# The row of scores stored word by word, and eight more state products in single passes, in a four-layer graph network under a planned order

## The chip, the cores and the metric

The kernel runs on one core of one Trainium2 chip. The metric is the device time of one execution in microseconds (us).

## The reference

There are 32 graphs of 512 nodes with 128 features each, and one weighted adjacency `adj` of 512 x 512 that all of them share. Four layers follow each other, each as x = x + layer(relu(layernorm(x))):

```python
# layer 0: normalised graph convolution
A = adj + eye;  d = A.sum(-1) ** -0.5
x = x + ((d[:, None] * A * d[None, :]) @ h) @ W.T + b
# layer 1: gated graph network, 5 steps
m_in = m_out = adj @ h;  av = concat(m_in, m_out);  u3 = h @ u3_w.T + u3_b
z = sigmoid(av @ w3.T + b3 + u3);  r = sigmoid(av @ w4.T + b4 + u3)
hv = tanh(av @ w5.T + b5 + (r * h) @ u5.T + u5b)
h = (1 - z) * h + z * hv
# layers 2 and 3: graph attention (elu after layer 2)
h = x @ W;  e = leaky_relu((h @ a_src)[:, None] + (h @ a_dst)[None, :], 0.2)
x = x + softmax(where(adj > 0, e, -inf)) @ h
```

All arithmetic is float32.

## The kernel before

**Order.** Nothing is scheduled by the compiler. The kernel first describes its work as some thousands of operations, each with an engine, an estimated cost, a delay until its result can be used, the values it reads and writes, and a due time (`op(engine, cost, due, emit, r, w, delay)`). `Plan.run` then simulates six queues (PE, DVE, ACT, POOL, SP, and ACT's DMA queue). In `attempt`, whenever an engine comes free, the ready operation with the earliest time that finds its buffers is started. The order in which operations were started is the order in which they are emitted. The times come from the due times or from a pass backwards (`ends` holds pairs of a last time and a factor for that), and `nudge` shifts them by pseudo-random amounts, one set for each number in the list `NUDGES`. On the chip every engine works through its own instructions in that order, and waits for semaphores where something is not there yet.

**Stages.** A graph b starts at due time 5 b (in units of one step); up to `LANES = 6` graphs are in the gated network at once, so layers 0, 1, 2 and 3 of different graphs overlap all the time. A tile of one graph is [128 partitions, 4 blocks, 128].

**Exact products from single passes.** A float32 matmul is an exact product (L829, function `weigh`), two records in the trace for 512 columns. Where `split` holds, an operand is cut into `upper` (ACT, L686), `lower` (DVE, L687) and `across` (DVE, L689) by `operands`, and the product is the sum of three matmuls in fp32r (L713 for adj, L832 for the gates), with a rescaling of the bank by ACT between two of them (L695). In `step`, the product of the state hT with the gate weight u3 is done this way for the pairs (batch, step) of `STATE_GATES`, and exactly for the others.

**Transposed copies.** States and features are turned by DVE in blocks of 32 x 32 (`sq`, L664 and L674) and rearranged by a shuttle through DRAM: four stores of 32 partitions (L667, L676) and a load (L669, L679), all issued from SP. Results are added onto x by accumulating DMAs from POOL (L658).

**Attention** (`gat`). Two pairs of matmuls (L962) give, for each node, 128 features and three scores; ACT takes the exponentials of the scores into columns D to D+2 of the tile `h_gat` (L978), then scales the features by column D (L982). The last column, D+2, holds what every destination node needs from every source node, and must become one row of 512 numbers that is the same on all partitions. For the 28 batches before the last four ("near") that goes through DRAM: DVE transposes the last 32 columns of `h_gat` into `four` (L998), one DMA stores one row out of every 32 partitions to `line` in DRAM (L1000), and a second loads `line`, broadcast over 128 partitions, into `row` (L1002). Then DVE builds the attention weights `e` (L1005, four per graph and layer) from row, column D+1 and the mask, and TensorE mixes (L1031). The near batches make their row on TensorE (L992) and mix at L1017.

The functions that the diff touches, with their line numbers:

Of the kernel before, what the change touches and what calls it, by code (L numbers as in the profile page):

```python
# [16 lines left out]
P = 128  # L17
# [3 lines left out]
W = 32  # L21
Q = P // W
# [5 lines left out]
RUN_UP = 8  # L28
LANES = 6
WHOLE_GATES = {(0, 0), (1, 0)}  # L30
STATE_GATES = {(b, s) for b in range(2, 32) for s in (1, 2, 3) if s > 1 or b % 4 == 1}

NUDGES = (
    53937, 420269, 836905, 654738, 2556, 688223, 875681, 275050, 155096, 344911, 330173, 435081, 694231, 213763,
    619624, 447574, 890946, 78316, 123147, 852796, 311235, 532539, 705019, 644762, 122001, 254734, 428857,
    882175, 724559, 991387, 688947, 809908, 194618, 494830, 529850, 799901, 343325, 398127, 50886, 241542,
    734658, 18633, 943566, 750849, 361157, 207391, 729651, 26139, 37696, 408480, 215591, 995383, 816582, 584268,
    494753, 34361, 342059, 302953, 168035, 239750, 279141, 68953, 280704, 389122, 194085, 766091, 380916,
    187191, 889942, 112078, 155070, 333073, 736484, 517839, 70535, 334845, 651590, 758394, 921455, 429200,
    648202, 752373, 775521, 430492, 606178, 231202, 882688, 679159, 354420, 928437, 520287, 661997, 81128,  # L40
    762603, 72380, 63081, 983120, 327354, 210125, 648122, 266391, 656086, 635831, 781379, 551997, 170768,
    229958, 7605, 122665, 19790, 73379, 142730, 998949, 708013, 923384, 153267, 690409, 481837, 535551, 726547,
    6387, 549650, 56134, 483951, 926497, 198992, 426418, 278155, 699450, 83978, 319322, 141756, 196198, 650583,
    862777, 201601, 166009, 204473, 988478, 570561, 164420, 526913, 618467, 275849, 776494, 261229, 110220,
    498182, 380461, 378001, 220860, 670765, 118796, 827070, 785629, 894747, 990151, 807156, 873672, 718913,
    239396, 50887, 63051, 862147, 532718, 800211, 505997, 9798, 801159, 13694, 618014, 193111, 44188, 893667,
    599496, 714567, 888600, 835938, 364887, 158288, 309678, 793120, 699620, 516755, 592013, 992036, 487540,
    190584, 971338, 58993, 486501, 268529, 250721, 557238, 569064, 166944, 933806, 390862, 463360, 136662,
    215430, 595978, 384591, 96926, 326923, 708222, 859934, 514585, 669817, 296375, 269747, 738262, 834297,
    459159, 608570, 133902, 490320, 941827, 144497, 573319, 819458, 309171, 845111, 880350, 927808, 432234,  # L50
    556385, 655493, 972795, 866892, 892882, 338341, 731096, 806800, 593721, 754374, 280850, 287395, 593450,
    812363, 340434, 322205, 340551, 845735, 66582, 645768, 736844, 878238, 109388, 497625, 999333, 437014,
    859840, 92294, 458622, 403652, 881921, 496809, 361450, 302403, 643048, 262383, 321316, 875159, 728173,
    763887, 249514, 200508, 52886, 149934, 537415, 299931, 655951, 358934, 513673, 678761, 726703, 828099,
    359414, 939210, 916234, 209320, 71814, 960653, 167324, 81204, 557783, 235008, 861486, 815903, 314980,
    593693, 811661, 356673, 912853, 833145, 889341, 728473, 302959, 14483, 119625, 907405, 192404, 98679, 42557,
    675297, 874633, 738462, 562610, 653446, 648327, 99334, 956314, 305909, 318958,
)


# [29 lines left out]
class Plan:  # L90
# [13 lines left out]
    def op(self, engine, cost, due, emit, r=(), w=(), delay=None):  # L104
        o = Op(engine, cost, due, emit, self.DELAY[engine] if delay is None else delay)
        o.id = len(self.ops)
        before = {}
        for items, writes in ((r, False), (w, True)):
            for item in items:
                v, parts = item if isinstance(item, tuple) else (item, None)  # L110
                parts = range(len(v.writers)) if parts is None else [parts]
                if v not in o.vals:
                    o.vals.append(v)
                    v.uses += 1
                for c in parts:
                    before.update((p.id, p) for p in v.writers[c])
                    if writes:
                        before.update((p.id, p) for p in v.readers[c])
        for items, writes in ((r, False), (w, True)):
            for item in items:  # L120
                v, parts = item if isinstance(item, tuple) else (item, None)
                for c in range(len(v.writers)) if parts is None else [parts]:
                    if writes:
                        v.writers[c], v.readers[c] = [o], []
                    else:
                        v.readers[c].append(o)
        before.pop(o.id, None)
        for p in before.values():
            p.then.append(o)
        o.waits = len(before)  # L130
        self.ops.append(o)
# [190 lines left out]
def gnn_stack(ctx: ExitStack, tc: tile.TileContext, a: dict, out: bass.AP):  # L322
    nc = tc.nc
    x, adj = a["x"], a["adj"]
    B, N, D = x.shape
    C = N // P
# [6 lines left out]
    def tiles(n, shape, name, pool=sb, dtype=F32):  # L333
        return [pool.tile(shape, dtype, name=f"{name}_{next(serial)}") for _ in range(n)]

    def flat(t):
# [19 lines left out]
        "hv": tiles(0, TOKENS, "hv"),  # L356
        "gT": tiles(0, [P, Q, W * C], "gT"),
        "h_gat": tiles(3, [P, C, D + 3], "h_gat"),
        "four": tiles(2, [P, Q, W], "four"),
        "row": tiles(2, [P, N], "row"),  # L360
        "line": tiles(4, [C, Q, W], "line", dram),
        "e": tiles(2, [P, C, N], "e"),
# [7 lines left out]
        "rstd": tiles(8, SMALL, "rstd"),  # L370
        "off": tiles(6, SMALL, "off"),
        "rden": tiles(3, SMALL, "rden"),
    }, [(167, 0.1), (181, 0.05)], 12,
        IDLE_FROM, lambda v: nc.tensor.transpose(v.t[:, 0, :], ident.t, ident.t))
    op = plan.op
    MM, MM1, TURN, MR = 0.858, 0.224, 0.111, 0.2325
# [44 lines left out]
    for c in range(C):  # L421
        e, q = (("ACT", nc.scalar), ("SP", nc.sync))[c % 2]
        op(e, 0.45, -1001, lambda c=c, q=q: q.dma_start(adj_sb.t[:, c, :], adj[c * P:(c + 1) * P, :]),
           w=[adj_sb[c]], delay=(3.2, 4.7, 4.4, 4.9)[c])
# [42 lines left out]
    for m in range(C):  # L467
        op("DVE", 0.26, -800 + 0.7 * m, lambda m=m: nc.vector.tensor_add(diag.t[:, m, :], block(adjT.t, m), ident.t),
           r=[adjT, ident], w=[diag[m]])
# [63 lines left out]
    for k, u, half in (("w4", "u3", True), ("w3", "u3", True), ("w5", "u5", False)):  # L533
        gate_b[k] = fixed([P, 1], "gate_b" + k)
        op("DVE", 0.1, -14, lambda k=k, u=u: nc.vector.tensor_add(gate_b[k].t, raw["b" + k].t, raw["b" + u].t),
           r=[raw["b" + k], raw["b" + u]], w=[gate_b[k]])
# [4 lines left out]
    for i, l in enumerate((2, 3)):  # L541
        p = Val("bank")
        op("PE", 0.3, 9, lambda i=i, l=l, p=p: nc.tensor.matmul(p.t[:, 0, :2], gats.t[:, i, :], a_pair[l].t, start=True, stop=True),
           r=[gats, a_pair[l]], w=[p])
# [138 lines left out]
    def operands(src, given, made, due):  # L683

        upper, lower, across = Val("upper"), Val("lower"), Val("across")
        op("ACT", COPY, due - 5, lambda: nc.scalar.mul(made(upper.t), given(src.t), BELOW), r=[src], w=[upper])  # L686
        op("DVE", V, due - 5, lambda: nc.vector.tensor_sub(made(lower.t), given(src.t), made(upper.t).bitcast(F32)),  # L687
           r=[src, upper], w=[lower])
        op("DVE", V, due - 5, lambda: nc.vector.scalar_tensor_tensor(  # L689
            flat(across.t), flat(lower.t).bitcast(F32), -SPLIT, flat(upper.t).bitcast(F32), op0=ALU.mult, op1=ALU.add),  # L690
           r=[lower, upper], w=[across])
        return upper, lower, across
# [131 lines left out]
    def step(b, s, m, hT, due, lane):  # L824
# [44 lines left out]

        if split and (b, s) in STATE_GATES:  # L870
            by_m(gate, 1, due + 0.2, True, parts=operands(hT, flat, flat, due))
# [69 lines left out]
    def gat(b, l, due):  # L941
        xb, y, gT, h = xs[b], Val("y", C), Val("sq"), Val("h_gat", 4)
# [13 lines left out]
        for a, q in enumerate(qs):  # L956
# [20 lines left out]
            else:  # L977
                op("ACT", 0.1, due + 1, lambda qt=qt, ht=ht: nc.scalar.activation(ht()[:, :, D:D + 3], qt()[:, :, D:D + 3], AF.Exp),  # L978
                   r=[q], w=[h[2 + a]])
# [4 lines left out]
        exps = [h[2], h[3]]  # L984

        row, e, mask = Val("row"), Val("e", C), (own_mask if near else maskT)[l]
        if near:
            pr = Val("bank")

            def spread():  # L990
                for k in range(Q):
                    nc.tensor.transpose(pr.t[:, k, :], h.t[:, k, D + 2:D + 3].to_broadcast([P, P]), ident.t)  # L992
            op("PE", C * TURN, due + 2, spread, r=[*exps, ident], w=[pr, e])
            row = pr
        else:

            four, line = Val("four"), Val("line")
            op("DVE", 0.2, due + 1.5, lambda: nc.vector.transpose(  # L998
                four.t, h.t[:, :, D + 3 - W:]), r=[h], w=[four])
            op("SP", 0.4, due + 1.5, lambda: nc.sync.dma_start(  # L1000
                line.t, four.t[W - 1::W]), r=[four], w=[line], delay=2.5)
            op("SP", 0.4, due + 1.5, lambda: nc.sync.dma_start(  # L1002
                row.t, line.t.rearrange("c q i -> (c q i)").unsqueeze(0).to_broadcast([P, N])), r=[line], w=[row, e], delay=7)
        for j in range(C):
            op("DVE", 0.661, due + 3, lambda j=j: nc.vector.scalar_tensor_tensor(  # L1005
                e.t[:, j, :], matrix(row), h.t[:, j, D + 1:D + 2], mask.t[:, j, :], op0=ALU.max, op1=ALU.mult),
               r=[row, h[2 + j // 2], mask], w=[e[j]])
# [4 lines left out]
        if near:  # L1012
# [7 lines left out]
            for js, cs in [([j], range(C)) for j in range(2 if apart else C)] + [((2, 3), [c]) for c in range(C if apart else 0)]:  # L1020
                op("PE", len(js) * len(cs) * MM1, due + 4, lambda js=js, cs=cs: mix_from(js, cs),
                   r=[part for j in js for part in (e[j], h[j // 2], h[2 + j // 2])], w=[*ps] if len(js) == 1 else [ps[cs[0]]])
# [36 lines left out]
        elif l == 2:  # L1059
            op("ACT", 0.505, due + 4, lambda: nc.scalar.activation(flat(n.t), flat(v.t), AF.Exp, bias=-1.0), r=[v], w=[n])  # L1060
            op("DVE", V, due + 4, lambda: nc.vector.scalar_tensor_tensor(flat(v.t), flat(n.t), 1.0, flat(v.t), op0=ALU.min, op1=ALU.max),  # L1061
               r=[n], w=[v])
# [13 lines left out]
    def attention(pair):  # L1076
        for b in (pair, pair + 1):
            gat(b, 2, STEPS * b + LANES * (STEPS - 1) + 3)
            gat(b, 3, STEPS * b + LANES * (STEPS - 1) + 8)
# [46 lines left out]
```

## Time and profile before

| | |
|---|---|
| median of 3 runs | 1486.99 us (1486.86 to 1487.59) |
| the profiled execution | 1487.39 us, of which span 1485.6 us |
| granted TensorE clock | 1.00 |
| idle of TensorE, VectorE, ScalarE, GpSimd in the span | 7.5, 79.4, 214.1, 823.1 us |
| DMA packets | 307,502, 196 MB |

The span is from the first to the last instruction of the profiled execution; 1.8 us lie around it. PE is TensorE's matmuls, PEld its weight loads, which overlap them; DVE is VectorE, ACT ScalarE, POOL GpSimd, SP the engine that issues most DMAs, and SPq its queue. A group's line gives source line, engine, operation, what is written and read, shapes and count, then busy time and the mean of one, and the engine's idle time just before, with what ended it. A wait's line has the waiter, the one waited for, then total us, times and the longest. A chain's line has start, length and what ran.

### The profile page before, as it was taken

The numbers are of one execution on the slowest core, as the hardware profiler recorded it, in microseconds if no ns is written. First come the engines' busy times: TensorE is split into PE (matmuls) and PEld (weight loads), VectorE is DVE, ScalarE is ACT, GpSimd is POOL, SyncE is SP. The second block draws the span as 40 slices with busy tenths as digits, with TensorE's granted clock in tenths as the row PEclk, the third lists the DMA queues.
The fourth block names the chain that finished last, engine by engine and source line by source line (L and its number), as shares of the span: only waits on it lengthen the run. The fifth ranks groups of instructions, "written<-read, shape, count | busy, mean of one in ns | idle before, by whom it ended". The sixth has DMA issues, their size and how long they took to land.

```text
span 1485.6 us, 25858 instructions
## 1 busy us (share of the span) xinstructions
PE 1478.1 (99%) x7481; PEld 1171.1 (79%) x7481; DVE 1406.2 (95%) x2951; ACT 1271.5 (86%) x2858; POOL 662.5 (45%) x1270
## 2 busy tenths in 40 slices
PE   9999999999999999999999999999999999999999
PEld 7777777787777788778778787877777877778888
DVE  8989999999998999899999999999999999999998
ACT  6978998888988888988889989799888889988874
POOL 5613641333755363655455553366536632414221
PEclk9999999999999999999999999999999999999999
DMA  3445555666766666666766557676576665553233
GB/s 107 65 104 144 108 127 117 139 142 159 154 136 134 156 156 138 139 142 138 178 138 145 134 128 153 143 173 139 127 162 154 148 158 122 136 135 74 70 79 79
DMA packets 307502, 196.12 MB, mean 132 GB/s; under 512 B 87872, under 2 KB 259232, under 8 KB 307360
## 3 DMA queue, kind: packets, MB, share of 16 engines
q1 hardware_dynamic: 276160, 157.24, 41.6%
q0 software_dynamic: 30912, 36.71, 16.3%
q8 instruction: 59, 0.97, 0.3%
q14 instruction: 83, 0.68, 0.2%
q10 hardware_dynamic: 288, 0.52, 0.1%
HBM read 87.30 MB, written 70.37 MB: 106 GB/s over the span
## 4 chain that ended last, share of the span: by engine, by line
PE 97%; DVE 1%; ACT 0%; DMA 0%; issue 0%; ACTq 0%; DVEq 0%
PE bank L713 35%; PE bank L832 26%; PE bank L829 15%; PE bank L1031 13%; PE bank L962 4%; PE bank L791 2%; PE bank L1017 2%; PE bank L736 1%; PE bank L653 0%; DVE e L1005 0%; DMA e<-in_adj_dram 0%; PE bank L507 0%; PE bank L992 0%; DVE st L630 0%; PE bank L455 0%
## 5 line engine op out<-in xcount | busy, mean ns | idle before, releaser
L695 ACT ACTIVATE bank<-bank 128x512 f32<-128x512 f32 x662 | 381.1, 598 | 92.4 <-PE bank L713 56.8
L689 DVE SCALAR_TENSOR_TENSOR across<-lower,upper 128x512 fp32r<-128x512 f32 x413 | 276.5, 678 | 2.2
L832 PE MATMUL bank<-upper,gates 128*128 128x512 f32 x541 | 257.2, 475 | 0.0
L1031 PEld LDWEIGHTS bank<-h_gat,e 128*128 128x128 f32 x1792 | 218.3, 191 | 17.6 <-issue 9.8
L1031 PE MATMUL bank<-h_gat,e 128*128 128x129 f32 x1792 | 220.5, 275 | 0.0
L832 PE MATMUL bank<-across,gates 128*128 128x512 f32 x541 | 218.3, 445 | 0.1
L832 PE MATMUL bank<-lower,gates 128*128 128x512 f32 x541 | 214.1, 396 | 0.0
L658 POOL DMA_DIRECT2D x<-y x80 | 72.1, 905 | 311.4 <-DVE y L1061 88.1
L713 PE MATMUL bank<-adj,upper 128*128 128x512 f32 x640 | 185.8, 412 | 0.0
L713 PE MATMUL bank<-adj,across 128*128 128x512 f32 x640 | 183.8, 411 | 0.0
L713 PE MATMUL bank<-adj,lower 128*128 128x512 f32 x640 | 172.7, 391 | 0.0
L829 PE MATMUL bank<-r,wT 128*128 128x512 f32 x320 | 163.3, 592 | 0.0
L1005 DVE SCALAR_TENSOR_TENSOR e<-row,h_gat,maskT 128x512 f32<-128x512 f32 x224 | 156.9, 741 | 0.0
L568 POOL TENSOR_TENSOR apart<-st 128x4 f32<-128x4 f32 x104 | 53.7, 517 | 218.1 <-DVE st L580 216.1
L713 PEld LDWEIGHTS bank<-adj,across 128*128 128x128 f32 x640 | 117.1, 188 | 36.6 <-issue 8.1
L713 PEld LDWEIGHTS bank<-adj,upper 128*128 128x128 f32 x640 | 117.8, 188 | 34.7 <-issue 10.3
L713 PEld LDWEIGHTS bank<-adj,lower 128*128 128x128 f32 x640 | 120.2, 188 | 26.6
L832 PEld LDWEIGHTS bank<-upper,gates 128*128 128x128 f32 x541 | 102.0, 188 | 42.5 <-issue 14.6
L832 PEld LDWEIGHTS bank<-across,gates 128*128 128x128 f32 x541 | 100.3, 188 | 41.1 <-issue 10.1
L874 ACT ACTIVATE r<-bank,gate_bw 128x512 f32<-128x512 f32 x160 | 111.4, 699 | 24.1 <-PE bank L829 21.4
L832 PEld LDWEIGHTS bank<-lower,gates 128*128 128x128 f32 x541 | 102.1, 189 | 37.8 <-issue 19.1
L568 POOL TENSOR_TENSOR rstd<-rstd,mhalf 128x4 f32<-128x4 f32 x104 | 128.1, 1232 | 5.1
(168 smaller groups left out, 3317.1 us busy)
## 6 DMA issues: line engine op xcount, KB each, us to landing
far<-sq SPq DMA_DIRECT2D x936, 64.0 KB
h<-far SPq DMA_DIRECT2D x148, 256.0 KB
x<-y POOLq DMA_DIRECT2D x80, 256.0 KB, 4.2
sq<-far SPq DMA_DIRECT2D x56, 256.0 KB
row<-line SPq DMA_DIRECT2D x56, 256.0 KB
adjT<-y POOLq DMA_DIRECT2D x32, 256.0 KB, 4.3
hT<-far SPq DMA_DIRECT2D x120, 64.0 KB
x<-in_x_dram SPq DMA_DIRECT2D x24, 256.0 KB
```

The costliest lines, as they stand in the source:

```text
L568: op("POOL", cost, due, lambda: nc.gpsimd.tensor_tensor(to(), one(), other(), how), r=r, w=w)
L658: op("POOL", 1.0, due, lambda: nc.gpsimd.dma_start(x.t, what(), accum_op=ALU.add), r=reads, w=[x], delay=7)
L689: op("DVE", V, due - 5, lambda: nc.vector.scalar_tensor_tensor(flat(across.t), flat(lower.t).bitcast(F32), -SPLIT, flat(upper.t).bitcast(F ...
L695: op("ACT", COPY, due, lambda: nc.scalar.mul(flat(p.t), flat(p.t), by), w=[p])
L713: nc.tensor.matmul(flat(p.t), left.t[:, c, :], right.t[:, c, :], start=first and c == 0, stop=c == C - 1, skip_group_check=True)
L791: nc.tensor.matmul(p.t[:, c, :], m.t[:, c, :], w0T.t[:, 0, :], start=True, stop=True)
L829: nc.tensor.matmul(flat(p.t), (of or gates).t[:, i, :], flat(moving.t), start=start, stop=True, skip_group_check=True)
L832: nc.tensor.matmul(flat(p.t), of.t[:, i, :], flat(moving.t), start=start, stop=True, skip_group_check=True)
L874: op("ACT", A, due - 5, lambda: nc.scalar.activation(flat(r.t), flat(gate.t), AF.Tanh, bias=gate_b["w4"].t, scale=0.5), r=[gate, gate_b["w ...
L962: nc.tensor.matmul(qt()[:, c, :D + 3], gT.t[:, 2 * a + c, :], w_aug[l].t, start=True, stop=True)
L1005: op("DVE", 0.661, due + 3, lambda j=j: nc.vector.scalar_tensor_tensor(e.t[:, j, :], matrix(row), h.t[:, j, D + 1:D + 2], mask.t[:, j, :], ...
L1031: nc.tensor.matmul(pt()[:, c, :D + 1], e.t[:, j, i * P:(i + 1) * P], h.t[:, j, :D + 1], start=(j == 0), stop=(j == C - 1))
```

## The change

Three things change in the text of the kernel.

1. `STATE_GATES` takes in step 1 of every odd batch, where it had every fourth: 75 pairs for 67.
2. In `gat`, for the batches that are not near, `four`, its buffers and the DVE transposition go. In their place four DMAs, one for each 32 partitions, read column D+2 straight from `h_gat` and store 128 single words each to a part of `line`. They need the exponentials alone, not the scaled features. The load of `row` is as it was, and waits for all four.
3. The planner's inputs: a store costs 0.44 and has a delay of 3, for 0.4 and 2.5; `ends` has one pair for two; `NUDGES` is another list, about half as long. So the order of the instructions differs on every engine.

```diff
-STATE_GATES = {(b, s) for b in range(2, 32) for s in (1, 2, 3) if s > 1 or b % 4 == 1}
+STATE_GATES = {(b, s) for b in range(2, 32) for s in (1, 2, 3) if s > 1 or b % 2}

 NUDGES = (
...
-        "four": tiles(2, [P, Q, W], "four"),
...
-    }, [(167, 0.1), (181, 0.05)], 12,
+    }, [(165.5, 0.090)], 12,
...
-            four, line = Val("four"), Val("line")
-            op("DVE", 0.2, due + 1.5, lambda: nc.vector.transpose(
-                four.t, h.t[:, :, D + 3 - W:]), r=[h], w=[four])
-            op("SP", 0.4, due + 1.5, lambda: nc.sync.dma_start(
-                line.t, four.t[W - 1::W]), r=[four], w=[line], delay=2.5)
+            line = Val("line", C)
+            for c in range(C):
+                op("SP", 0.44, due + 1.5, lambda c=c: nc.sync.dma_start(
+                    line.t[c].rearrange("q i -> i q"), h.t[c * W:(c + 1) * W, :, D + 2]), r=exps, w=[line[c]], delay=3)
             op("SP", 0.4, due + 1.5, lambda: nc.sync.dma_start(
                 row.t, line.t.rearrange("c q i -> (c q i)").unsqueeze(0).to_broadcast([P, N])), r=[line], w=[row, e], delay=7)
```

## The prediction

> **What bounds the kernel now.** I read the page first (busy shares, then the chain that ended last), then the stretches of time, then the groups of instructions.
>
> ```profile
> PE 1478.1 (99%) x7481; PEld 1171.1 (79%) x7481; DVE 1406.2 (95%) x2951; ACT 1271.5 (86%) x2858; POOL 662.5 (45%) x1270
> PE 97%; DVE 1%; ACT 0%; DMA 0%; issue 0%; ACTq 0%; DVEq 0%
> 0.00:50.00 50.00, 47.02 (x250) 36.55 (x250) 44.69 (x162) 37.20 (x81) 30.03 (x75) 1.00 0.34 90
> 1300.00:1400.00 100.00, 100.00 (x509) 78.86 (x508) 96.13 (x188) 85.56 (x192) 26.07 (x49) 1.00 0.41 100
> 1400.00:1440.00 40.00, 39.06 (x279) 34.41 (x278) 36.20 (x110) 31.48 (x94) 13.24 (x25) 1.00 0.31 73
> 1440.00:1486.00 46.00, 42.08 (x377) 41.79 (x375) 40.72 (x136) 24.62 (x88) 7.47 (x7) 1.00 0.28 70
> ```
>
> In the stretch lines the columns are the stretch, its length, then busy time and count of PE, PEld, DVE, ACT and POOL, granted clock, DMA share, GB/s. TensorE is idle 7.5 us in the whole span: 3.0 in the first 50, 0.9 in 1400 to 1440, 3.9 at the very end, and practically nothing between. The chain says the same: 97% is TensorE. Since busy ends of matmuls are modelled, I count as well. The chain has "81 us: 16 passes in 3.73 us", 0.233 us a pass of 512 columns:
>
> ```profile
> 80.96 3.73 PE bank L713 x16
> 711.97 0.23 PE bank L832
> 712.20 0.86 PE bank L829 x2
> 713.06 0.45 PE bank L962 x4
> ```
>
> There are 2,256 + 1,623 single passes (L713, L832), x 0.233 = 904 us; 518 records of L829, two to a product of 0.86, make 222; the other 3,058 records (3,026 at 0.11, 32 wider) make 349. The sum, 1,475, leaves 10.6 us of the 1485.6 for every gap, seven of them at the two ends. So only two things can move the time: TensorE's own work, and new gaps in it. Nothing that frees another engine is worth anything by itself.
>
> **What the Trainium skill says.** "FP8 and Floating Point Precision", TensorE Precision Notes: true FP32 takes four passes through the array. The trace agrees: 0.86 us for a product at L829 against 0.233 for a single pass, a ratio of 3.7. "DMA: Bandwidth & Descriptors", Rules for kernel authors: a non-contiguous last dimension lowers to one descriptor per element. No transfer of scores in this trace is of that kind, so only the new one will show it. The same page, Anatomy of one DMA, puts most of a fixed 2 us down to the receipt of the write; here the row copy follows the issue of its store by 1.6 us at the least and 2.8 in the median (56 pairs, from start times). "TensorE: Matmul & The Clock Gate", specifications: VectorE's queue is strictly first in, first out; in the trace it shows as stalls of whatever stands first (27.7 us of L687 behind L686).
>
> **Part 1, eight more state products in single passes.** STATE_GATES grows from 67 to 75 entries: step 1 of batches 3, 7, 11, 15, 19, 23, 27 and 31. Each loses one exact product and gains three single passes plus the split of hT.
>
> ```profile
> L829 PE MATMUL bank<-hT,wT 128*128 128x512 f32 x186 | 94.9, 592 | 0.0
> L686 ACT ACTIVATE upper<-hT 128x512 fp32r<-128x512 f32 x67 | 43.6, 653 | 1.9 <-DVE hT L890 1.9
> L687 DVE TENSOR_TENSOR lower<-hT,upper 128x512 fp32r<-128x512 f32 x67 | 45.3, 678 | 0.9 <-ACT upper L686 0.9
> L998 DVE STREAM_TRANSPOSE four<-h_gat 128x128 f32<-128x128 f32 x56 | 16.7, 298 | 2.9 <-ACT h_gat L982 2.9
> L1005 DVE SCALAR_TENSOR_TENSOR e<-row,h_gat,maskT 128x512 f32<-128x512 f32 x224 | 156.9, 741 | 0.0
> ```
>
> TensorE: 8 x (0.86 - 3 x 0.233) = 8 x 0.16 = **1.3 us less**, all of it on the path. ScalarE: 8 x 0.653 = 5.2 us more, on an engine with 214 us idle. VectorE: 16 splits x 0.678 = 10.8 us more (L687, L689). The rescaling of the bank is there already and isn't doubled. The first half of the gate now waits for a three-step split, about 2 us when nothing queues, before its passes; the other five lanes and the attention products cover that, as they do for the 67 splits of today: TensorE's waits before L832 for L687 and for L689 come to 0.5 us each. If that cover goes, up to 2 us x 8 = 16 us; I take 0, both ends kept.
>
> **Part 2, the row of scores.** Removed: 56 VectorE transpositions, 16.7 us, and the wait of the transposition on both scalings (2.9 us). VectorE in sum: 1406.2 + 10.8 - 16.7 = 1400.3 us, 6 less. Worth 0 on the path, as TensorE doesn't wait for VectorE. On SP, 56 stores of 0.500 us go (28 us) and 224 of one word per descriptor come. The nearest row is the shuttle's store, also 128 descriptors, 0.438 us in the median: 98 us. SP's issue records sum to 697 us, and become 767 of 1485.6. What SP loses as well is its wait on the transposition:
>
> ```profile
> SPq L1000 <- DVE four L998: 81.3, 22, 12.9
> SPq L1002 <- DMA line<-four: 22.4, 18, 2.6
> L1000 SPq DMA_DIRECT2D line<-four x56: 487/500/747, 216.0 to 1447.8; - x56
> ```
>
> Behind those 81.3 us stand the shuttle's transfers (L667, L669) that bring the states back, so a shorter wait is a help to them; four stores in place of one hold them up 4 x 0.438 - 0.5 = 1.25 us per row. Both fall inside the shuttle's slack, since waits for DMA hardly occur on the compute engines, and count 0. POOL's accumulating transfers only take other places; POOL is idle 55% of the span.
>
> The DMA engines get 56 x 512 = 28,672 packets of 4 bytes. The trace's packets of 128 bytes took 13.2 ns each and its 4-byte semaphore writes 9.1. At 13.2 it is 378 us over 16 engines, 24 us each, 1.6% of the span on engines busy some 58% in all. If a word cost as much as a 512-byte packet (31.5 ns), it would be 3.8%. Both are covered.
>
> How late does the row come? Before: issue 0.5, at least 1.6 to the row copy. After: issue 1.75 in all, then the last store's landing, which no row shows: between 1.1 us (as now, 1.6 less the 0.5 of issue) and, as a bound, 5 us, twice the longest wait that L1002 now has for it (2.6). It starts earlier by the scaling and the transposition: the store follows the second exponential (L978) by 2.3 us in the median, and that can fall to nothing. Before 2.3 + 1.6 = 3.9 us, after 1.75 + 1.1 = 2.9 to 1.75 + 5 = 6.8: between 1 us earlier and 2.9 us later. I take 0. Today L1005 has 0.0 us of idle before it, and starts 8.0 us (median; 4.9 at least) after the row copy is issued.
>
> **Part 3, other due times.** They redraw the order on all engines. With 10.6 us of gaps in all, of which about 3 are start and 4 are the last VectorE steps and stores, at most some 3 us are to be had, and any amount to be lost. I take 0, with -2 to +8.
>
> **Sum.** 1487.4 (the profiled execution: span 1485.6 and 1.8 around it) - 1.3 = 1486.1. The median of the three runs, 1486.99, is 0.4 below that execution: **1485.7**.
>
> **The cases.**
>
> A, 53%: as summed, order as tight as now: 1485.7, own range 1484 to 1489. For it: TensorE has no gap from 50 to 1400 us to begin with, and both engines that could starve it get no more work than they had, or little.
>
> B, 17%: the row arrives after the place where the order has L1005, VectorE stalls with everything behind it, and VectorE becomes the bound. Its room is 1484.3 - 1400.3 = 84 us, 1.5 us per row. A mean stall over 1.5 us decides; at 1.65, within the bounds above, 92 us of stalls give 84 + 8 over: 1485.7 + 8 = 1494. Against it: 4.9 us between copy and use at the worst today.
>
> C, 20%: the new order is looser, and splits come late for their passes (part 1). Of the bound of 16 us a third gives 5: 1485.7 + 5 = 1490.7, which I take; half gives 1493.7. It decides from 4.3 us of new gaps on. Against: the 67 splits of today work unseen.
>
> D, 10%: the new order also closes 1.5 to 2 us at the ends, 1483.9. For it: 0.9 us idle in 1400 to 1440 needn't be there. Against: the ends hang on first loads and last stores.
>
> That the change does less than it says can be left out: all eight pairs pass the condition in step() that chooses the split, and the counts would show it.
>
> **Numbers.** About 0.2% (3 us) is what a measurement of this kernel can tell from no change. Faster by more than that needs under 1484.0: D nearly whole and a sliver of A, 0.12. Slower means over 1490.0: B, most of C and A's rim, 0.35. The rest, 0.53, is no difference. The range runs from 1483.5 to 1494.5, leaving out the far ends of B, C and D.
>
> **What would show it.** Right: L829 for hT x170 instead of x186, L832 groups x549 each, no L998; TensorE busy all through 50 to 1400; span about 1484.3; L1005 still with no idle. Case B: idle before L1005 released by a DMA row. Case C: idle before L832 or L713 released by ScalarE or VectorE. I am wrong in kind if TensorE's counts are as said and the span moves by more than 3 us.

## The result, and the profile after

The changed kernel takes 1623.3 us (median of 4 runs, 1617.9 to 1628.8) against 1487.2 of the kernel before: a ratio of 1.0916, 95% interval 1.0889 to 1.0942. That is 136 us slower, far outside the range of the prediction. The profiled execution took 1621.3 us, its span 1619.5.

From the page of the changed kernel, the engines' busy times, the DMA count, and the chain that ended last by engine and by line:

```profile
PE 1522.4 (94%) x7487; PEld 1189.0 (73%) x7487; DVE 1407.9 (87%) x2911; ACT 1278.7 (79%) x2866; POOL 643.6 (40%) x1270
...
DMA packets 339311, 196.14 MB, mean 121 GB/s; under 512 B 119904, under 2 KB 291040, under 8 KB 339168
...
PE 41%; DMA 26%; ACT 13%; DVE 10%; SPq 6%; issue 3%; DVEq 0%; ACTq 0%
PE bank L701 14%; PE bank L820 10%; DMA line<-h_gat 7%; DMA h<-far 7%; PE bank L817 6%; DMA far<-sq 5%; PE bank L1018 5%; DMA sq<-far 5%; ACT bank L683 3%; ACT upper L674 2%; PE bank L950 2%; SPq L655 2%; SPq L987 2%; DVE lower L675 2%; DVE e L992 2%
```

Every engine is busy for a smaller share of the span than before. TensorE is idle for 97.1 us of the span where it was idle for 7.5, and busy for 44 us more. TensorE's share of the chain fell from 97% to 41%, and a quarter of the chain is now transfers: the new word stores (`line<-h_gat`, 7%) and, with more weight together, the three kinds of the shuttle that the change didn't touch. From the view of waits of the changed kernel, first the compute engines', then SP's own queue (waiter, waited for, us in total, times, longest):

```profile
ACT upper L674 <- DMA h<-far: 57.3, 24, 6.2
PE bank L950 <- DMA sq<-far: 39.6, 17, 6.9
DVE sq L652 <- DMA far<-sq: 31.9, 14, 6.7
DVE e L992 <- DMA row<-line: 22.0, 13, 5.5
```

```profile
SPq L989 <- DMA line<-h_gat: 136.4, 57, 6.6
SPq L655 <- DMA line<-h_gat: 33.5, 20, 4.0
SPq L664 <- DMA line<-h_gat: 17.7, 9, 3.2
```

Before, L1002 waited 22.4 us for its store; the same copy, now L989, waits 136.4. From the list of DMA issues of the changed kernel (KB of each, median us from issue to landing):

```profile
far<-sq SPq DMA_DIRECT2D x936, 64.0 KB, 2.8
line<-h_gat SPq DMA_DIRECT2D x224, 0.5 KB, 7.1
```

A store of 512 bytes in single words takes 7.1 us to land (the trace tells the landing of 31 of the 224), where a store of 64 KB takes 2.8. The planner was told 3 for it.

The first reading of this was theory S: the words land late, the row copy waits for them on SP, and everything behind it on that queue is late. Its rivals: theory E, the words hold up the DMA engines for every transfer, whoever waits; theory O, the new order is bad in itself. The experiments keep the changed kernel's order of instructions wherever they can, because the order alone turned out to be worth tens of us.

### The profile page after: what moved, and what is told of

The parts are those of the page before. It is cut to its first block, busy times and chain, and to the rows that moved or that the text cites. A ratio compares the mean times of both kernels' runs of the same rounds, so it can differ in the third digit from the quotient of the medians.

```text
span 1619.5 us, 25988 instructions
## 1 busy us (share of the span) xinstructions
PE 1522.4 (94%) x7487; PEld 1189.0 (73%) x7487; DVE 1407.9 (87%) x2911; ACT 1278.7 (79%) x2866; POOL 643.6 (40%) x1270
## 4 chain that ended last, share of the span: by engine, by line
PE 41%; DMA 26%; ACT 13%; DVE 10%; SPq 6%; issue 3%; DVEq 0%; ACTq 0%
PE bank L701 14%; PE bank L820 10%; DMA line<-h_gat 7%; DMA h<-far 7%; PE bank L817 6%; DMA far<-sq 5%; PE bank L1018 5%; DMA sq<-far 5%; ACT bank L683 3%; ACT upper L674 2%; PE bank L950 2%; SPq L655 2%; SPq L987 2%; DVE lower L675 2%; DVE e L992 2%
## 5 line engine op out<-in xcount | busy, mean ns | idle before, releaser
L677 DVE SCALAR_TENSOR_TENSOR across<-lower,upper 128x512 fp32r<-128x512 f32 x421 | 281.8, 679 | 3.2 <-PE bank L701 0.7
L820 PE MATMUL bank<-upper,gates 128*128 128x512 f32 x549 | 262.6, 478 | 7.8 <-ACT bank L683 4.3
L820 PE MATMUL bank<-across,gates 128*128 128x512 f32 x549 | 226.2, 455 | 5.4 <-ACT bank L683 5.1
L820 PE MATMUL bank<-lower,gates 128*128 128x512 f32 x549 | 221.9, 404 | 7.6 <-DVE lower L675 7.4
L1018 PE MATMUL bank<-h_gat,e 128*128 128x129 f32 x1792 | 223.9, 276 | 2.1 <-DVE e L992 1.4
L701 PE MATMUL bank<-adj,upper 128*128 128x512 f32 x640 | 193.7, 425 | 5.6 <-ACT upper L674 5.6
L992 DVE SCALAR_TENSOR_TENSOR e<-row,h_gat,maskT 128x512 f32<-128x512 f32 x224 | 156.5, 742 | 22.2 <-DMA row<-line 22.0
L675 DVE TENSOR_TENSOR lower<-h,upper 128x512 fp32r<-128x512 f32 x158 | 107.2, 679 | 53.1 <-ACT upper L674 51.8
L674 ACT ACTIVATE upper<-h 128x512 fp32r<-128x512 f32 x158 | 100.7, 638 | 62.7 <-DMA h<-far 57.3
L820 PEld LDWEIGHTS bank<-upper,gates 128*128 128x128 f32 x549 | 105.5, 192 | 52.7 <-issue 14.9
L820 PEld LDWEIGHTS bank<-lower,gates 128*128 128x128 f32 x549 | 105.5, 192 | 51.3 <-issue 18.2
```

Of the source, the lines that this page charges most:

```text
L701: nc.tensor.matmul(flat(p.t), left.t[:, c, :], right.t[:, c, :], start=first and c == 0, stop=c == C - 1, skip_group_check=True)
L820: nc.tensor.matmul(flat(p.t), of.t[:, i, :], flat(moving.t), start=start, stop=True, skip_group_check=True)
L1018: nc.tensor.matmul(pt()[:, c, :D + 1], e.t[:, j, i * P:(i + 1) * P], h.t[:, j, :D + 1], start=(j == 0), stop=(j == C - 1))
```

## The experiments

**1. The row copy doesn't wait.**

```diff
 op("SP", 0.4, due + 1.5, lambda: nc.sync.dma_start(
-    row.t, line.t.rearrange("c q i -> (c q i)").unsqueeze(0).to_broadcast([P, N])), r=[line], ...
+    row.t, adj[0:1, :].to_broadcast([P, N])), r=[line], ...
```

> The changed kernel, its order of instructions untouched on every engine; only the row copy reads a line of the adjacency in DRAM instead of the stored scores, so it no longer waits for the word stores (the scores are left out of the attention weights). All 224 word stores are still issued. Theory S (the single words land late, 7.1 us where the order allows 3.4, and the row copy that waits for them holds up everything behind it on SP): 136 us of SP's waits go, and the time falls by at least half of the 136 us of loss, to 1490 to 1555; what is left are the 75 us in which other transfers wait for the word stores. Theory E (the words clog the 16 DMA engines for all transfers): it stays over 1590. Theory O (the new order is bad in itself): it stays over 1590.

Measured: 1636.0 us (1631.9 to 1640.1; ratio 1.0999, 1.0966 to 1.1031). Nothing came back, though the row copy hardly waits any more. But its wait went in part to others. From SP's waits of experiment 1:

```profile
SPq L655 <- DMA line<-h_gat: 60.4, 34, 5.2
SPq L989 <- DMA line<-h_gat: 12.5, 11, 4.2
```

In sum SP waits 121 us for word stores, where it waited 211. So the wait of the row copy falls as the main cause; that SP is held up at other places by the late words isn't excluded by this run.

**2. Few words.**

```diff
-    line.t[c].rearrange("q i -> i q"), h.t[c * W:(c + 1) * W, :, D + 2]), r=exps, ...
+    line.t[c].rearrange("q i -> i q")[:1], h.t[c * W:c * W + 1, :, D + 2]), r=exps, ...
```

> The changed kernel in the same order, but each store takes 1 partition instead of 32: 4 words in place of 128, 16 in place of 512 a row (most of the row is left at values filled in once, by four extra transfers after about 105 us). The 224 issues on SP and the row copy's wait remain. Theories S and E: a store of few words lands in about 2 to 3 us, and the time is 1484 to 1500. Theory O, or one in which SP is burdened by the number of issues: it stays over 1590.

Measured: 1495.4 us (1492.7 to 1498.2; ratio 1.0054, 1.0038 to 1.0070). The same issues, the same waits, the same order, and 128 us less. So it is the words themselves, and not the order or the number of SP's issues. (An issue is even longer here, 0.562 us in the median for 0.432.)

**3. The transposition put back** (L998 to L1000 of the kernel before in place of the four stores; the other edits of the change stay).

> The changed kernel (75 state products, its list and its end) with the row made by VectorE's transposition and one store again. Every operation's number shifts, so the planner's small shifts fall on other operations and the order is a third one. Theories S and E: 1484 to 1500. Theory O (list, end or the 75 products cost the time): over 1550.

Measured: 1532.8 us (ratio 1.0316, 1.0299 to 1.0333). Between the two expectations: the words' loss is gone, and 46 us remain. Experiments 7 and 11 take this up.

**4. The planner told of the late landing** (`delay=7` for `delay=3`).

> The changed kernel with one number of the planner changed: the word stores' delay is 7 instead of 3 us, about what the trace shows from issue to landing. The work is the same, the order leaves time between store and row copy. Theory S: the waits on SP go and the time is 1488 to 1520. Theory E: the engines are as clogged as before, over 1570. Theory O: no statement, since the order changes.

Measured: 1658.9 us (ratio 1.1152, 1.1130 to 1.1175). With time planned between store and copy, the kernel is slower still. By experiment 3 a new order can cost some 40 us by itself, and the row copy still waits 65.3 us for the words, for 136.4; so this tells only that the room didn't help. It fits E and doesn't prove it.

**5 and 6. Where the words go.** Both start from experiment 1. In the one, the words go to an SBUF tile; in the other, to DRAM, but each 512 bytes from the next.

```diff
-    "line": tiles(4, [C, Q, W], "line", dram),
+    "line": tiles(4, [P, Q], "line"),                   # 5: line.t[c * W:(c + 1) * W] is written
+    "line": tiles(4, [C, Q, W, P], "line", dram),       # 6: line.t[c][:, :, 0] is written
```

> As the run in which the row copy reads the adjacency (1636 us), with the same order on every engine; but the 512 words of a row are stored into a small SBUF tile instead of DRAM (the scores are left out of the attention weights as there). Theory E1 (it is the writing of single words to DRAM that holds the DMA engines): 1484 to 1505. Theory E2 (any transfer of 128 descriptors of one word is slow, by its reads or its count): over 1590.

> As the run in which the row copy reads the adjacency (1636 us), with the same order; but each word goes to a place of its own in DRAM, 512 bytes from the next, where it was 4 bytes. Theory E1a (the engines collide, because 16 of them write words of the same 512 bytes at once): the time falls to 1484 to 1520. Theory E1b (each single word is a slow write to DRAM wherever it goes): it stays over 1590.

Measured: 1500.7 us to SBUF (ratio 1.0087, 1.0058 to 1.0116), 1490.8 us spread (1.0021, 1.0014 to 1.0028), against 1636.0. The second is the decisive one: the same number of words, descriptors, issues and waits, in the same order, into the same memory, and 145 us less. Words to DRAM aren't slow; words side by side are. (To SBUF an issue took 0.599 us on SP for 0.431, which may be a part of the 10 us between the two runs; that wasn't tried.) Once the words are apart they land in a median of 1.5 us, from the list of DMA issues of experiment 6:

```profile
far<-sq SPq DMA_DIRECT2D x936, 64.0 KB, 1.9
...
line<-h_gat SPq DMA_DIRECT2D x224, 0.5 KB, 1.5
```

And the untouched stores of the shuttle land in 1.9 where they took 2.8 in the changed kernel; of SP's waits for word stores nothing is left. How the words hurt transfers that nobody made wait for them can be seen at the first row, where the two runs issue the same transfers at the same times. From the timeline of SP in experiment 1, then in experiment 6 (start, length, what):

```profile
212.85 2.02 SPq L987 DMA_DIRECT2D line<-h_gat  x4
215.03 0.34 SPq L657 DMA_DIRECT2D h<-far  x1
217.19 0.30 SPq L655 DMA_DIRECT2D far<-sq  x1
```

```profile
212.81 2.04 SPq L987 DMA_DIRECT2D line<-h_gat  x4
215.01 0.34 SPq L657 DMA_DIRECT2D h<-far  x1
217.17 0.30 SPq L655 DMA_DIRECT2D far<-sq  x1
```

and from the stretches of time, again experiment 1 and then 6 (the last two columns are the DMA engines' busy share and the GB/s, both of the packets that start in the stretch):

```profile
216.00:217.00 1.00, 1.00 (x6) 0.82 (x5) 1.00 (x2) 1.00 (x4) 0.00 (x0) 1.00 0.38 33
217.00:218.00 1.00, 1.00 (x6) 0.77 (x6) 1.00 (x3) 1.00 (x4) 0.00 (x0) 1.00 0.24 16
```

```profile
216.00:217.00 1.00, 1.00 (x6) 0.81 (x5) 1.00 (x2) 1.00 (x4) 0.00 (x0) 1.00 0.66 156
217.00:218.00 1.00, 1.00 (x6) 0.79 (x5) 1.00 (x3) 1.00 (x4) 0.00 (x0) 1.00 0.32 119
```

The load `h<-far` is issued at 215.0 in both. In experiment 6 it flows in the next two microseconds at 156 and 119 GB/s: the packet records have all its 128 packets of 2 KB started by 217.5. Behind packed words only 33 and 16 GB/s move, 24 such packets have started by 218, and the engines' records show them idle most of the time. Yet the words' own packets are all recorded by 215.7, in both runs. So the engines stand still with their next work at hand.

Nor is it only SP's queue that stands. GpSimd issues its transfers itself, whatever SP waits for. From the lists of experiments 1 and 6:

```profile
x<-y POOLq DMA_DIRECT2D x80, 256.0 KB, 4.9
```

```profile
x<-y POOLq DMA_DIRECT2D x80, 256.0 KB, 4.2
```

Sorted by time, of all GpSimd's transfers whose landing the trace tells, those issued between 2 us before and 3 us after the issue of a word store land in a median of 8.0 us in experiment 1 (28 of them), the other 76 in 4.7. In experiment 6 it is 4.8 and 4.4. So the words hold up transfers that go by another queue and wait for nothing on SP: this is theory E. It doesn't show in packet time, as 4-byte packets are recorded at 9 ns in either run. That the engines are held until the words' writes are completed is the likely reading; no record shows it directly. How much of the loss is this hold, and how much SP's 121 us of waits, isn't separated.

**7. The kernel before with an empty list** (`NUDGES = ()`).

> The kernel before with an empty NUDGES list: the same work and data paths, an order without the shifts. This measures what an order is worth that has not been fitted to just this set of operations, as the rows of the run with the transposition put back (1533 us) need it. If the 46 us of that run are the order alone, this one is slow by a like amount, 1505 to 1540. If they come from the 75 products or the new end, this one stays under 1495.

Measured: 1501.9 us (ratio 1.0095, 1.0066 to 1.0124). The order's worth is real but, at 14 us, less than expected; it doesn't by itself account for the 46 of experiment 3, whose list fell on other operations than it was made for.

**8, 9 and 10. How near is too near.** All from experiment 1 with the row copied from the adjacency.

```diff
+    "line": tiles(4, [C, Q, W, 16], "line", dram),   # 8:  line.t[c][:, :, 0], words 64 bytes apart
+    "line": tiles(4, [C, W, P], "line", dram),       # 9:  line.t[c][:, :Q], 4 neighbours, partitions 512 bytes apart
+    "line": tiles(4, [C, W, Q], "line", dram),       # 10: line.t[c], 4 neighbours, partitions 16 bytes apart
```

> As the run with the words 512 bytes apart (1490.8 us), same order, row copied from the adjacency; but the words lie 64 bytes apart. If words collide only within stretches of 64 bytes or less: 1487 to 1497, landing in 1.5 us. If the stretch in which they collide is 512 bytes: eight words share it, and the time lies between, over 1500.

> As the run with the words 512 bytes apart, but the four words of a partition lie side by side (16 bytes), and the partitions 512 bytes apart. [...] If only the words of different engines hold each other up: 1487 to 1497, landing 1.5 to 2 us. If successive words of one engine do as well: landing over 2.5 us and a time over 1500.

> As the last, but the partitions follow each other without a gap: the same 512 bytes per store as in the changed kernel, only that the words of one partition are neighbours and not 128 bytes apart. If what counts is how many words of how many engines meet in 512 (or 64) bytes: over 1580 (or over 1510), as in the changed kernel. If neighbouring words of one engine merge: under 1500.

Measured: 1491.8 us at 64 bytes (1490.7 to 1494.2; ratio 1.0025, 1.0014 to 1.0036), so 64 bytes of distance are enough (landing 1.7 us, for 1.5 expected). 1497.3 us with four neighbours (1.0066, 1.0043 to 1.0089), between the two outcomes expected: the landing is over 2.5 us, the time under 1500. 1741.5 us for neighbours packed without a gap (1.1702, 1.1668 to 1.1736), the worst of all. From the views of the tile `line` of experiments 6, 8 and 9, in this order:

```profile
DMA to landing us min/median/max: 1.4/1.5/5.1
```

```profile
DMA to landing us min/median/max: 1.4/1.7/5.1
```

```profile
DMA to landing us min/median/max: 1.4/2.8/6.0
```

Four words in one stretch cost 1.3 us over one. If each of the three others takes its turn, that is about 0.43 us apiece; an estimate for the changed kernel, where 16 words fall into every 64 bytes, is 1.5 + 15 x 0.43 = 8.0 us, against 7.1 measured. That words take turns is argued from this, not shown, and the count alone doesn't decide: experiment 10 has 16 words in every 64 bytes too, and is over 100 us slower than experiment 1. Words of different partitions aren't needed for the effect, as in experiment 9 the four words of a stretch come from one partition; which DMA engine carries which word no view shows. Why packed neighbours are worse than the changed kernel's pattern, where a partition's four words lie 128 bytes apart, isn't settled; the trace has no landings there, and the issues took 0.598 us for 0.431.

**11 and 12. The changed order without the words, and the eight products alone.** In 11, the row is made complete again inside the changed kernel's order:

```diff
+    def put(c, line=line):
+        if c == C - 1:
+            four = fours[0]
+            fours.reverse()
+            nc.vector.transpose(four, h.t[:, :, D + 2:D + 3].to_broadcast([P, Q, W]))
+            nc.sync.dma_start(line.t, four[W - 1::W])
     for c in range(C):
-        op("SP", 0.44, due + 1.5, lambda c=c: nc.sync.dma_start(...), r=exps, w=[line[c]], delay=3)
+        op("SP", 0.44, due + 1.5, lambda c=c, put=put: put(c), r=exps, w=[line[c]], delay=3)
```

In 12, on top of it, for step 1 of batches 3, 7, ... 31 the passes of the state's parts are left out of `first_two` and `third_one`, and `weigh(p, 0, hT, of=gates)` is issued instead.

> The changed kernel's order and its 75 products, with the row made on VectorE again, and complete: where the last of the four word stores stood, VectorE turns the column D+2 (each value read 32 times, so the scalings are not waited for) and SP issues one store of 4 x 512 bytes; the other three issues go. The planner doesn't know of the transposition. If the single words are the whole loss of the change: 1484 to 1492, no longer measurably apart from the kernel before or nearly so. If order, list, end or products cost something of their own: over 1494.

> As the run beside it, with the same order of operations, but the eight products that the change made single-pass are exact again on TensorE (85 + 8 exact ones); their splits on ScalarE and VectorE are still done and left unused. This measures the first part of the change alone. By its own sum (8 x (0.86 - 3 x 0.233)) it takes 1.3 us more than the run beside it, 0.5 to 2. If the products are hidden by other gaps of TensorE: no difference. If the extra passes' waits cost more than they save: it is faster.

Measured: 1490.9 us (16 runs, 1489.3 to 1495.3; ratio 1.0022, 1.0015 to 1.0030) and 1494.0 us (5 runs, 1492.8 to 1494.8; ratio 1.0039, 1.0025 to 1.0053). So the eight products in single passes are worth 3.1 us by the medians, with one of the 16 runs lying above all of the other kernel's; more than the 1.3 of their passes and than the 0.5 to 2 expected. Part of it are gaps: in the profiled executions TensorE's busy time differs by 1.7 us, the spans by 3.9. Experiment 11 also settles experiment 3: same products, end and list and a like path for the row, 42 us apart, so those 42 are the order (but for one difference: the transposition of experiment 3 waits for the scalings, that of 11 doesn't).

No version here beats the kernel before.

## Why the prediction was wrong

**The ledger.** 1623.3 - 1487.2 = 136.1 us. Of this, 1623.3 - 1490.9 = 132.4 are the word stores (experiment 11), in agreement with 128 from experiment 2 and 145 from 1 and 6. The remaining 3.7 are the products' gain of about 3 and, by difference, 6 to 7 of loss for the rest, the new order above all.

**The bound: right.** TensorE was the limit, and in experiment 6 it is again:

```profile
PE 1478.5 (99%) x7487; PEld 1173.3 (79%) x7487; DVE 1402.7 (94%) x2911; ACT 1273.6 (86%) x2866; POOL 661.6 (44%) x1270
```

VectorE's 1402.7 stand beside a forecast of 1400.3. The step "only two things can move the time: TensorE's own work, and new gaps in it" held as well: of 134 us of span, 90 are new gaps and 44 are longer busy time of TensorE. The prediction's count left out 26 records of 0.11 us; with them the passes make 1,478 and leave 7.7 us of gaps for 10.6, next to the 7.5 of idle time. Nothing hangs on it. What the prediction named as the sign of being wrong in kind came: TensorE's counts as said, and a span that moved by more than 3 us.

**Part 1: right in sign, the size too small.** About 3 us by the medians (experiments 11 and 12) for 1.3. The counts are as said. From the groups of the changed kernel:

```profile
L817 PE MATMUL bank<-hT,wT 128*128 128x512 f32 x170 | 90.2, 613 | 3.8 <-DMA hT<-far 3.8
L820 PE MATMUL bank<-upper,gates 128*128 128x512 f32 x549 | 262.6, 478 | 7.8 <-ACT bank L683 4.3 <-ACT upper L674 3.1 <-DVE lower L675 0.4
```

**Part 2: here it failed, by counting the word stores at 0 where they cost 132 us.** SP's issue was priced well: 0.432 us in the median for 0.438 forecast. The packets too: 31,809 more in all, of which 28,672 are the words by count (56 x 512), one descriptor per element as the Trainium skill says ("DMA: Bandwidth & Descriptors", Rules for kernel authors).

The first step that failed is the landing, "between 1.1 us ... and, as a bound, 5 us", for 7.1 measured. It was scaled from the store of before, four runs of 512 bytes, and from SP's longest wait for that; nothing in the trace of before showed how 128 words packed into 512 bytes land. The fixed 2 us that the prediction quoted from the same page of the Trainium skill (Anatomy of one DMA) are given there for transfers issued from GpSimd; the word stores are issued from SP, and the 7.1 us measured stand in their place.

The second is the step "At 13.2 it is 378 us over 16 engines ... Both are covered". It took the duration of a packet's record for the engine's time. The records of 4-byte packets come to 220 us before and 524 after, 19 us more on each of 16 engines, so that sum was fair; but after the words the engines stand longer than their packets are recorded (experiments 1 and 6).

From that followed the third error, "Both fall inside the shuttle's slack ... and count 0". The reason given was that the compute engines hardly waited for DMA. That shows that the shuttle was in time, not by how much, and how much was never measured; with the words it was late.

**The rivals.** Case B had the right cause, words that land slowly, but the wrong place: the place named, L1005 (now L992), waits only 22 us, and VectorE is 87% busy, so it is no bound. What is late are the shuttle's transfers: ScalarE waits 57 us before L674 for `h<-far`, VectorE 32 before L652, and TensorE itself 40 before L950; most of TensorE's other waits are for what ScalarE and VectorE then deliver late. No case had the transfers of others as the victim, so the range ended at 1494.5.

**Part 3: inside its bounds.** About +6 to +7 by difference, for -2 to +8; that it is the order is inferred.

The granted clock was 0.98 in the changed kernel, where it was 1.00 before and in experiment 6; that adds to TensorE's busy time (1522 for 1478 us). An estimate from the clock of 0.981 is 1477 / 0.981 = 1506, so 29 us of the rise; the rest stays open. The clock is lower where there are more gaps: 1.00 where TensorE is 99% busy, 0.998 at 98% (experiment 3), 0.98 at 94%, 0.947 at 89% (experiment 10). That the gaps lower the clock is not shown.

## What to carry to other kernels

A DMA whose packets are recorded at 9 ns each may still hold up the DMA engines for microseconds: price a scattered store by its landing and by what other transfers do meanwhile, and where no row of the profile shows its pattern of addresses, keep the upper bound wide. Don't let single words be written side by side into DRAM; gather them on an engine first (here 0.3 us of VectorE), or space them out (a load that collects spaced words again wasn't tried: in all those runs the row copy read the adjacency). And where an order is fitted to its set of operations, compare variants inside one order, or the order's own 14 to 42 us will hide what is asked.

## What the runs showed of the hardware that was not expected

Single words written to DRAM by DMA hold each other up when they lie side by side, and not at 64 bytes apart. The 128 words of a store landed in a median of 1.5 us at 512 bytes apart, 1.7 at 64 bytes, 2.8 with four neighbours in 16 bytes, and 7.1 packed; to SBUF, four neighbours in each of 32 partitions landed in 1.8 us. After packed words the DMA engines also move little else: 33 and 16 GB/s for 156 and 119 with the same load waiting, and transfers that GpSimd issued near them landed in 8.0 us for 4.7. Distances between 4 and 64 bytes weren't tried.
